# Two triples side by side in the first product of a ConvNeXt block, with another order of loads, pads and norms

## The chip, the cores and the metric

The kernel runs on one core of one Trainium2 chip. The metric is the device time of one execution in microseconds (us); smaller is better. Times of the kernel before are given as the median of three runs.

## The reference

All data are fp32. The input x is (32, 384, 28, 28): 32 images (here called blocks, b), C = 384 channels, 784 pixels. Two layers follow each other:

```python
# layer 0: ConvNeXt block
y = depthwise_conv_7x7(x, dw_w) + dw_b            # padding 3
y = layernorm over the 384 channels of a pixel
y = gelu(y @ w1 + b1)                             # 384 -> 1536, exact gelu
gx = sqrt(sum over pixels of y * y)               # per image and feature
nx = gx / (mean of gx over the features + 1e-6)
y = grn_g * (y * nx) + grn_b + y                  # GRN
x = x + (y @ w2 + b2)                             # 1536 -> 384
# layer 1: a gate for each channel
avg, mx, mn = mean, max, min of x over the pixels
logits = concat(avg @ W1.T, grouped(mx, W2_1) * W2_2, mn @ W3.T) @ Wfc.T
out = sigmoid(logits + x)
```

GRN needs the sum of squares over all pixels of a block before any of its features can be scaled, so within a block the second product has to wait for the whole first product.

## The kernel before

**Convolution stage (0 to 497.6 us).** x is read in 12 chunks of 32 channels. A chunk consists of eight pieces (`NG = 8`), each of 32 channels by 4 images: 128 partitions of 784 pixels, 0.4 MB. `load_x(i)` issues the load of piece i, `AHEAD = 6` pieces before it is needed. `pad_x(i)` copies it into a buffer with rows padded to 32 (GpSimd, L245). `turn_x` transposes the padded piece on TensorE (L256) and copies the transposes into the chunk's tile xt (VectorE L264, ScalarE L266). The convolution itself is a product of xt with a banded matrix per channel. These matrices are not stored: the DRAM table `fs` holds one short row per channel (written at the start, L200 and L207, on ScalarE's DMA queue), and `load_t(s)` (L211) reads it with a skewed access pattern into `tmat`, 8 channels per step s, 48 steps in all, four `tmat` buffers. TensorE makes `pc` from both (L393, L394, L397), VectorE (L403) and ScalarE (L411) add the bias `dwb` and write `yc`, which goes to DRAM (`yd`, `yl`). Beside each step the next chunk's pieces are padded and transposed. GpSimd also forms sums of weights in this stage and stores them in `u1d` and `u2d`.

**Products.** Both products use a bilinear scheme with 15 block products where a plain 3 x 3 x 2 product takes 18. The operands are blocks and sums of blocks: `forms_up` (L573) makes the sums for the first product, `forms` (L679) for the second, both on GpSimd after the first block. The table `UPSTEPS` lists the 15 steps of the first product: the operand, the weight sum, the PSUM bank, whether the bank is started anew, and what is done with the bank afterwards (a copy on ScalarE or an add, subtract or reversed subtract on VectorE). `up(b)` goes through four triples of 128-feature rows, `KT = 4`; a triple is 15 steps on two matmul instructions each (L607), and its six results (copies L614, sums L616 to L624) are the halves of three rows of y. It loads the triple's weights in one piece of 960 KB (L596), two buffers. `down(b)` is the second product: 15 steps of eight matmul instructions (L703), weights from L698, and VectorE adds each bank to x (L717, L719).

**What runs beside them.** Per block there are 12 `gelu` (L582), 12 `square` (L588) with the sums of squares, one `grn` (L637 to L649), 12 `scale` on ScalarE, and for the block that comes after next `turn`: for each of seven pixel tiles j a norm on ScalarE (`yn`, L515), three transposes on TensorE (`py`, L533), and after tiles 3 and 6 three evictions on ScalarE that apply the LayerNorm's weights (`acc`, L515). `stats` and `std` prepare the norms, `gate_store` (L738 to L757) does the gate of the block before.

**Order.** After `up(0)` and `up(1)` comes `down(0)`, and then `up(b + 1)` and `down(b)` alternate. A dictionary of hooks says at which step of a product another function is called. Within `up` a `gelu` stands after steps 3, 7 and 11 of a triple (for the triple before it) and a `square` after the same steps from the third triple on (for the one two before it). `beside(b)` gives the hooks of `down(b)`: the last three `gelu` at step 0, `turn` of b + 2 at steps 0 to 3, six `square` at 4 and 5, `stats`, `std` and `grn` at 8, `gate_store` and `load_x` at 9, the scales at 10 to 13, `forms` at 14. `start_hooks()` does the same for `up(0)` and `up(1)`. The order of the calls is the order of the instructions on each engine, and an engine takes its instructions in that order. SP issues nearly all loads and stores; ScalarE's queue issues the stores of `fs` and of `out`.

A step is defined like this:

```python
    ("z", "-12", "D", 1, (("D", "add", "2b"),)),
    ("0b", "-10+11", "A", 0, (("A", "copy", "1b"), ("D", "rsub", "1b"))),
```

Step z writes bank D, which VectorE adds to the half row 2b; step 0b goes on in bank A, which ScalarE copies to 1b, and then VectorE subtracts 1b from bank D.

Of the kernel before, what the change touches and what calls it, by code (L numbers as in the profile page):

```python
# [89 lines left out]

UPSTEPS = (
# [8 lines left out]
    ("z", "-12", "D", 1, (("D", "add", "2b"),)),  # L100
    ("0b", "-10+11", "A", 0, (("A", "copy", "1b"), ("D", "rsub", "1b"))),
    ("0a", "-00", "B", 0, (("B", "sub", "0a"),)),
    ("t", "+00+10-11", "H", 1, (("H", "add", "E"),)),
    ("q", "-00+01+02-10+11", "A", 0, (("A", "plus", "0b"),)),
    ("u", "+00+10+12", "B", 0, (("B", "minus", "1a"),)),
    ("2b", "-12-20+21+22", "F", 1, (("F", "add", "2b"),)),
)
KT = FB // 3

# [10 lines left out]
def convnext_gate_kernel(  # L120
# [26 lines left out]
    fs = dram.tile([C + 1, FL], F32, name="fs")  # L147
# [28 lines left out]
    with ExitStack() as one:  # L176
        tp = one.enter_context(tc.tile_pool(name="tp", bufs=1))
        xip = one.enter_context(tc.tile_pool(name="xip", bufs=6))
# [21 lines left out]
        nc.scalar.dma_start(fs[C : C + 1, :], tab[:1, 0, :])  # L200
        for cb in range(CB):
            nc.vector.tensor_copy(
                tab[:, cb, S0 : S0 + SN - 7].rearrange("p (y x) -> p y x", x=PW)[:, :, :7],
                dww[:, cb, :42].rearrange("p (y x) -> p y x", x=7),
            )
            nc.vector.tensor_copy(tab[:, cb, S0 + SN - 7 :], dww[:, cb, 42:])
            nc.scalar.dma_start(fs[cb * P : (cb + 1) * P, :], tab[:, cb, :])  # L207
        NK = C // TC

        def load_t(s, eng=nc.sync):  # L210
            eng.dma_start(  # L211
                tmat[s % NT2].rearrange("p c m -> p (c m)"),
                bass.AP(
                    tensor=fs.tensor,
                    offset=fs.offset + s * TC * FL,
                    ap=[[1, P], [1, TC * FL]],
                ),
            )
# [25 lines left out]
        def pad_x(i):  # L244
            nc.gpsimd.tensor_copy(  # L245
                xpad[i % NPAD][:, :, :HW], xis.pop(i).rearrange("p (r w) -> p r w", w=HW)
            )
# [80 lines left out]
        AHEAD = 6  # L328
# [3 lines left out]
        for i in range(NG):  # L332
            pad_x(i)
            if i == NG - AHEAD:
                load_t(0)
            if i == NG // 2:

                nc.gpsimd.tensor_copy(tmat[1][:, 0, :1], xpad[i % NPAD][:, 0, :1])
                load_t(1)
                nc.sync.dma_start(dwb, cvec[0:1, :].broadcast_to([P, C]))  # L340
            if i + AHEAD < GT:
                load_x(i + AHEAD)
            for h in range(2):
                turn_x(i, h, xt, (nc.vector, nc.scalar)[h])
# [116 lines left out]
    up1 = ctx.enter_context(tc.tile_pool(name="up1", bufs=2))  # L461
# [15 lines left out]
    ssqs, gscs, gates, ys, ops = {}, {}, {}, {}, {}  # L477
# [39 lines left out]
    def turn(b, j, norm=nc.scalar, evac=(nc.scalar,) * CB):  # L517

        rstd, nmr = sts[b]
        h = j // 4  # L520
        if j == 0:

            pool, tag = (xp, "x") if b == 1 else (accp, "acc")
            accs[b] = pool.tile([P, CB, NT], F32, tag=tag, name=f"acc_{b}")
        if j % 4 == 0:
            pts[b] = [bank(f"py_{b}_{h}_{cb}") for cb in range(CB)]
        yn = ynp.tile([P, C], F32, tag="yn", name=f"yn_{b}_{j}")
        affine(
            norm, yn.rearrange("p (k c) -> p k c", c=YC), yis[b][:, :, j, :],
            rstd[:, j : j + 1], nmr[:, j : j + 1],  # L530
        )
        for cb in range(CB):
            nc.tensor.transpose(  # L533
                pts[b][cb][:, j % 4 * P : (j % 4 + 1) * P], yn[:, cb * P : (cb + 1) * P], ident
            )
        if j % 4 < 3 and j < NJ - 1:
            return
        for cb in range(CB):
            affine(
                evac[cb],  # L540
                accs[b][:, cb, h * 4 * RW * HW : (j + 1) * RW * HW].rearrange(
                    "p (r w) -> p r w", w=HW
                ),
                pts[b][cb][:, : (j % 4 + 1) * P]
                .rearrange("p (j q) -> p j q", q=P)[:, :, ::-1]
                .rearrange("p j (r w) -> p j r w", w=PW)[:, :, :, :HW],
                lng_t[:, cb : cb + 1],
                lnb_t[:, cb : cb + 1],
            )
# [40 lines left out]
    def up(b, hooks, squares=True):  # L590
# [3 lines left out]
        for t in range(KT):  # L594
            wt = up1.tile([P, NS, P], F32, tag="u1", name=f"u1_{b}_{t}")
            nc.sync.dma_start(wt, u1d[t])  # L596
            banks = {}
            z = {
                f"{m}{'ab'[h]}": ym[:, 3 * t + m, h * NH : (h + 1) * NH]
                for m in range(3)  # L600
                for h in range(2)
            }
            z["E"] = tep.tile([P, NH], F32, tag="te", name=f"te_{b}_{t}")
            for i, (opnd, _, bk, first, acts) in enumerate(UPSTEPS):
                if first:
                    banks[bk] = bank(f"ph_{b}_{t}_{bk}")
                nc.tensor.matmul(  # L607
                    banks[bk][:, :NH], wt[:, i, :], o[opnd],
                    start=(first == 1), stop=True, skip_group_check=True,
                )  # L610
                for src, how, to in acts:
                    p, d = banks[src][:, :NH], z[to]
                    if how == "copy":
                        nc.scalar.activation(d, p, AF.Identity)  # L614
                    elif how == "add":
                        nc.vector.tensor_tensor(d, d, p, ALU.add)  # L616
                    elif how == "sub":
                        nc.vector.tensor_tensor(d, d, p, ALU.subtract)  # L618
                    elif how == "rsub":
                        nc.vector.tensor_tensor(d, p, d, ALU.subtract)  # L620
                    elif how == "plus":
                        nc.vector.tensor_tensor(d, p, z["E"], ALU.add)  # L622
                    else:
                        nc.vector.tensor_tensor(d, p, z["E"], ALU.subtract)  # L624
                if i in (3, 7, 11):
                    m = (i - 3) // 4
                    if t >= 1:
                        gelu(b, 3 * (t - 1) + m)
                    if t >= 2 and squares:
                        square(b, 3 * (t - 2) + m)  # L630
                run(hooks, (t, i))
# [131 lines left out]
    def beside(b):  # L763
# [4 lines left out]

        n = b + 1
        last = n == B - 1  # L770
        if n < B:
            for m in range(3):
                at(0, gelu, n, FB - 3 + m)
# [6 lines left out]
        if n < B:  # L780
            f0 = 0 if b == 0 else FB - 6
            for i in range(f0, FB):
                at((i - f0) // 3 if last else 4 + (i - f0) // (2 if b else 4), square, n, i)
        if b + 3 < B:
            at(8, stats, b + 3)
            at(8, std, b + 3)
        if n < B:
            at(2 if last else 8, grn, n)
        if b >= 1 and not last:
            at(9, gate_store, b - 1)  # L790
        if n < B:
            at(9 if b else 0, load_x, n)
        if n < B:
            for f in range(FB):
                at((2 if last else 10) + f // 3, scale, n, f)
            if last:
                at(6, forms, n, 0, 4)
                at(9, forms, n, 4, EARLY)
            else:
                at(NS - 1, forms, n, 0, EARLY)  # L800
        if b >= 1 and last:
            at(7, gate_store, b - 1)
        return hooks

    def start_hooks():
        h0, h1 = {}, {}

        def at(h, t, i, fn, *args):  # L810
            h.setdefault((t, i), []).append(lambda: fn(*args))

        V, A = nc.vector, nc.scalar
        if B > 1:
            at(h0, 0, 8, stats, 1)
            at(h0, 0, 8, std, 1)
            for j in range(NJ):
                at(h0, 1, 1 + 2 * j, turn, 1, j, V)
            at(h0, 1, NS - 1, forms_up, 1)
        if B > 2:  # L820
            at(h0, 2, 6, load_y, 2)
        for m in range(3):
            at(h1, 0, 1 + 2 * m, gelu, 0, FB - 3 + m)
        for i in range(6):
            at(h1, i // 5, (8, 10, 11, 12, 13, 0)[i], square, 0, FB - 6 + i)
        if B > 2:
            at(h1, 0, 5, stats, 2)
        at(h1, 1, 1, grn, 0)
        if B > 2:
            at(h1, 1, 1, std, 2)  # L830
        for f in range(FB):
            at(h1, 1 + (6 + f) // 12, (6 + f) % 12, scale, 0, f, A if f % 2 else V)
        at(h1, 2, 8, forms, 0, 0, EARLY)
        return h0, h1

    h0, h1 = start_hooks()
    stats(0)
    std(0)
    for j in range(NJ):
        turn(0, j, (nc.scalar, nc.vector)[j % 2], (nc.scalar, nc.vector, nc.scalar))  # L840
    forms_up(0, nc.vector)
    if B > 1:
        load_y(1)
    up(0, h0)
    load_x(0)
    if B > 1:
        up(1, h1, squares=False)
    else:
        for fs in h1.values():
            for fn in fs:  # L850
                fn()
    for b in range(B):
        if b >= 1 and b + 1 < B:
            up(b + 1, {})
# [41 lines left out]
```

## Time and profile before

| | |
|---|---|
| Time, median of 3 runs | 3168.45 us (3166.55 to 3168.86) |
| Profiled execution: time | 3168.3 us |
| Profiled execution: span | 3166.6 us |
| Busy in the span: PE, DVE, ACT, POOL | 3125.4, 1685.1, 1878.7, 1616.9 us |
| Convolution stage | 0 to 497.6 us |
| Change of stage | 497.6 to 512.5 us |
| One steady block | 82.57 us: first product 40.32, second product 42.25 |

PE is TensorE's matmul, PEld its weight load, DVE is VectorE, ACT is ScalarE, POOL is GpSimd, and SP issues transfers. L12 is line 12 of the kernel. The page of the profile gives busy time per engine, the chain of work that ended last, and groups of instructions. A stage window sums one stretch of time: for each engine the sum of durations and the number of instructions, then the granted TensorE clock (1.00 is full), the mean busy share of the DMA engines, and what they moved in GB/s. A timeline lists single instructions or runs of like ones: start in us from the span's start, duration in us, engine, line, operation, output <- inputs, shape, and xN for a run of N. What stands in brackets at its end is idle time of the engine ahead of it, with what ended it.

### The profile page before, as it was taken

To read this page: it belongs to the slowest core of one execution; us is meant where nothing else is said; L and a number is where in the kernel's file an instruction comes from. 1 tells how busy PE (TensorE), PEld (TensorE's weight loads), DVE (VectorE), ACT (ScalarE), POOL (GpSimd) and SP (SyncE) were. 2 spreads that over 40 slices of the span, in tenths; PEclk is the share of its full clock that TensorE was granted. 3 is DMA by queue.
4 is the path that set the end of the run, shared out by engine and by line. 5 is a ranking of instruction groups with operands and counts; after the bars stand their busy time and mean duration, and the time that the engine had idled before them with its cause. 6 is when DMAs were issued, how large, how long until landed. Compare 5 with 4: busy or idle time off the path is not lost.

```text
span 3166.6 us, 33843 instructions
## 1 busy us (share of the span) xinstructions
PE 3125.4 (99%) x11459; PEld 1978.5 (62%) x11459; DVE 1685.1 (53%) x3444; ACT 1878.7 (59%) x3032; POOL 1616.9 (51%) x853
## 2 busy tenths in 40 slices
PE   8999998999999999999999999999999999999998
PEld 7999996555555555555555555555555555555554
DVE  3443436555555555555555555555555555555554
ACT  2222225866677766666666666666666666677762
POOL 2453421555555555555555555555555555555555
PEclk9999999999999999999999999999999999999999
DMA  9989985434444444444444444444444444444333
GB/s 346 356 311 395 348 302 191 132 114 143 143 144 142 134 137 145 143 136 148 148 136 148 145 138 147 136 148 148 148 130 137 132 145 144 143 142 144 127 102 131
DMA packets 257154, 540.73 MB, mean 171 GB/s; under 512 B 121022, under 2 KB 130775, under 8 KB 247767
## 3 DMA queue, kind: packets, MB, share of 16 engines
q1 hardware_dynamic: 244148, 500.70, 47.2%
q10 hardware_dynamic: 12834, 37.88, 3.1%
q8 instruction: 91, 1.49, 0.2%
q14 instruction: 81, 0.66, 0.1%
HBM read 447.53 MB, written 90.99 MB: 170 GB/s over the span
## 4 chain that ended last, share of the span: by engine, by line
PE 98%; DVE 1%; ACT 1%; DMA 1%; issue 0%; ACTq 0%; POOL 0%; POOLq 0%; SPq 0%; DVEq 0%
PE ph_A L607 14%; PE ph_B L607 13%; PE pz_A L703 11%; PE pz_B L703 11%; PE pz_C L703 5%; PE ph_C L607 5%; PE pz_E L703 5%; PE pc L393 5%; PE pc L394 4%; PE pc L397 4%; PE pz_F L703 3%; PE ph_D L607 3%; PE ph_H L607 3%; PE ph_F L607 3%; PE pz_G L703 3%; PE pz_D L703 3%
## 5 line engine op out<-in xcount | busy, mean ns | idle before, releaser
L582 ACT ACTIVATE y<-y,fv 128x784 f32<-128x784 f32 x384 | 346.8, 941 | 214.2 <-DVE y L622 213.5
L679 POOL TENSOR_TENSOR d_v<-d_u,y 128x1568 f32<-128x1568 f32 x32 | 112.3, 3509 | 661.2 <-PE pz_B L703 640.6
L515 ACT ACTIVATE y<-y,fv,gsc 128x784 f32<-128x784 f32 x378 | 358.7, 1027 | 30.1 <-DVE gsc L649 30.1
L588 ACT ACTIVATE junk<-y 128x784 f32<-128x784 f32 x384 | 326.6, 851 | 5.0
L411 ACT ACTIVATE yc<-pc,dwb 128x224 f32<-128x224 f32 x192 | 103.6, 641 | 367.4 <-PE pc L397 269.8
L607 PE MATMUL ph_A<-af,u 128*128 128x392 f32 x768 | 313.8, 503 | 5.4 <-DVE af L573 5.3
L607 PE MATMUL ph_B<-af,u 128*128 128x392 f32 x768 | 311.3, 493 | 0.3 <-ACT y L614 0.3
L703 PE MATMUL pz_A<-y,u 128*128 128x392 f32 x768 | 268.5, 492 | 0.0
L738 POOL TENSOR_TENSOR zt<-gate,st 128x96 f32<-128x96 f32 x32 | 11.2, 350 | 456.9 <-DVE st L726 456.9
L679 POOL TENSOR_TENSOR y<-d_v,y 128x1568 f32<-128x1568 f32 x64 | 223.5, 3514 | 2.4
L607 PEld LDWEIGHTS ph_A<-af,u 128*128 128x128 f32 x768 | 136.4, 190 | 135.2 <-ACT y L614 57.7
L607 PE MATMUL ph_A<-acc,u 128*128 128x392 f32 x512 | 216.3, 504 | 0.0
L393 PE MATMUL pc<-xt,tmat 128*128 128x224 f32 x768 | 209.4, 354 | 6.3 <-issue 4.5
L607 PE MATMUL ph_B<-acc,u 128*128 128x392 f32 x512 | 213.6, 499 | 0.0
L607 PEld LDWEIGHTS ph_B<-af,u 128*128 128x128 f32 x768 | 145.2, 190 | 109.0 <-DVE y L618 9.6
L703 PEld LDWEIGHTS pz_A<-y,u 128*128 128x128 f32 x768 | 145.8, 190 | 106.6
L245 POOL COPY xpad<-xi 128x784 f32<-128x784 f32 x96 | 80.5, 839 | 250.7 <-PE pt L256 178.6
L618 DVE TENSOR_TENSOR y<-y,ph_A 128x392 f32<-128x392 f32 x128 | 71.9, 562 | 238.3 <-PE ph_A L607 227.3
L504 ACT ACTIVATE sd<-mv,eps_t 128x7 f32<-128x7 f32 x32 | 9.6, 300 | 314.3 <-DVE mv L499 314.3
L614 ACT ACTIVATE y<-ph_A 128x392 f32<-128x392 f32 x256 | 123.9, 484 | 112.7 <-PE ph_A L607 112.6
L573 POOL TENSOR_TENSOR af<-af,acc 128x392 f32<-128x392 f32 x186 | 187.1, 1019 | 4.9
L397 PE MATMUL pc<-xt,tmat 128*128 128x192 f32 x768 | 187.6, 326 | 0.0
(157 smaller groups left out, 7043.1 us busy)
## 6 DMA issues: line engine op xcount, KB each, us to landing
u<-u1d SPq DMA_DIRECT2D x128, 960.0 KB, 4.7
u<-u2d SPq DMA_DIRECT2D x480, 256.0 KB, 2.6
tmat<-fs SPq DMA_DIRECT2D x48, 1420.0 KB, 11.2
yd<-yc SPq DMA_DIRECT2D x22, 1792.0 KB, 8.8
yi<-yd SPq DMA_DIRECT2D x32, 1232.0 KB, 6.5
xi<-in_x SPq DMA_DIRECT2D x96, 392.0 KB, 9.5
x<-in_x SPq DMA_DIRECT2D x32, 1176.0 KB, 6.1
out<-x ACTq DMA_DIRECT2D x31, 1176.0 KB, 5.1
```

Of the source, the lines that this page charges most:

```text
L393: nc.tensor.matmul(pc[:, ci, :N], t[:, c, P : 2 * P], xc, start=True, stop=False)
L394: nc.tensor.matmul(pc[:REACH, ci, : N - B], t[:, c, 2 * P : T0 + MW], xc[:, B:], start=False, stop=False)
L397: nc.tensor.matmul(pc[:, ci, B:N], t[:, c, :P], xc[:, : N - B], start=False, stop=True)
L411: nc.scalar.activation(yc[:, :, :, cy + ci].rearrange("p b j -> p j b"), pc[:, ci, :N].rearrange("p (j b) -> p j b", j=NJ), AF.Identity, b ...
L515: eng.activation(out, in_, AF.Identity, bias=add, scale=mul)
L573: eng.tensor_tensor(d, o[in0], o[in1], op)
L582: nc.scalar.activation(y, y, AF.Gelu, bias=b1_t[:, f : f + 1], scale=1.0)
L588: nc.scalar.activation(junk, ys[b][:, f, :], AF.Square, accum_out=ssqs[b][:, f : f + 1])
L607: nc.tensor.matmul(banks[bk][:, :NH], wt[:, i, :], o[opnd], start=(first == 1), stop=True, skip_group_check=True,)
L614: nc.scalar.activation(d, p, AF.Identity)
L679: nc.gpsimd.tensor_tensor(d, o[in0], o[in1], op)
L703: nc.tensor.matmul(pz[:, :NH], wt[:, t, :], o[opnd][:, t, :], start=(first == 1 and t == 0), stop=(t == KT - 1), skip_group_check=True,)
```

## The change

**Start of the convolution stage.** x is loaded eight pieces ahead, in eight buffers, where it was six. `fs` becomes three tables, one for each 128 channels, each with its own extra row; a `load_t` therefore depends on the stores to one table. The first `load_t` comes in two halves right after the first pad, with the load of `dwb` behind it, and the second `load_t` two pieces before the end of the first chunk. From the ninth piece on `pad_x` is an activation (Identity) on ScalarE.

```diff
-        xip = one.enter_context(tc.tile_pool(name="xip", bufs=6))
+        xip = one.enter_context(tc.tile_pool(name="xip", bufs=8))
...
-            nc.gpsimd.tensor_copy(
-                xpad[i % NPAD][:, :, :HW], xis.pop(i).rearrange("p (r w) -> p r w", w=HW)
-            )
+            if i < NG:
+                nc.gpsimd.tensor_copy(dst, src)
+            else:
+                nc.scalar.activation(dst, src, AF.Identity)
...
-        AHEAD = 6
+        AHEAD = NG
...
-            if i == NG - AHEAD:
-                load_t(0)
-            if i == NG // 2:
+            if i == 0:
+                load_t(0, 2)
+                nc.sync.dma_start(dwb, cvec[0:1, :].broadcast_to([P, C]))
+            if i == NG - 2:
```

**First product.** The steps of triples t and t + 1 alternate. Each of the two triples has three banks A, B and C: steps z, t and 2b, which had banks of their own (D, H and F), now go through C. The weights of a triple come in three loads of 5 steps (320 KB each), six buffers.

```diff
-    ("z", "-12", "D", 1, (("D", "add", "2b"),)),
-    ("0b", "-10+11", "A", 0, (("A", "copy", "1b"), ("D", "rsub", "1b"))),
+    ("z", "-12", "C", 1, (("C", "add", "2b"),)),
+    ("0b", "-10+11", "A", 0, (("A", "copy", "1b"), ("C", "rsub", "1b"))),
...
-    ("t", "+00+10-11", "H", 1, (("H", "add", "E"),)),
+    ("t", "+00+10-11", "C", 1, (("C", "add", "E"),)),
...
-    ("2b", "-12-20+21+22", "F", 1, (("F", "add", "2b"),)),
+    ("2b", "-12-20+21+22", "C", 1, (("C", "add", "2b"),)),
...
+        for t2 in range(0, KT, 2):
             for i, (opnd, _, bk, first, acts) in enumerate(UPSTEPS):
...
+                for t in (t2, t2 + 1):
+                    if i % UG == 0:
+                        wts[t] = up1.tile([P, UG, P], F32, tag="u1", name=f"u1_{b}_{t}_{i}")
+                        nc.sync.dma_start(wts[t], u1d[t, :, i : i + UG, :])
```

**What runs beside the products.** `norm` is split from `turn`; the norms of tiles 0 and 1 of block b + 1 are called within `up(b)`, near its end, and `turn` uses them later. The scales and the `forms` of a block leave the end of its `down` neighbour and are called in the first pair of triples of the next `up`. The first six `gelu` of a block stand in the second pair of triples, the other six in the first two steps of `down`, and the squares from step 3. `stats` stays at 8; `std` and `grn` go to 9, `gate_store` and `load_x` to 10. The first two blocks and the last have orders of their own.

```diff
+        else:
+            for i, f in enumerate(order):
+                at((0, 2 * i), scale, p, f)
+            at((0, 24), forms, p, 0, EARLY)
+        if b != 1:
+            for m in range(HF):
+                at((2, 2 + 4 * m), gelu, b, m)
+            for m in range(squared(b)):
+                at((2, 28 if m >= HF // 2 else 22 + 2 * m), square, b, m)
+        if 1 <= b and b + 1 < B:
+            for j in range(2):
+                at((2, 26 + 2 * j), norm, b + 1, j)
...
-            f0 = 0 if b == 0 else FB - 6
-            for i in range(f0, FB):
-                at((i - f0) // 3 if last else 4 + (i - f0) // (2 if b else 4), square, n, i)
+            g0 = 0 if n == 1 else HF
+            for f in range(g0, FB):
+                at((f - g0) // 3, gelu, n, f)
+            s0 = squared(n)
+            for f in range(s0, FB):
+                at((1 if last else 3) + (f - s0) // 2, square, n, f)
...
-            for f in range(FB):
-                at((2 if last else 10) + f // 3, scale, n, f)
-            if last:
-                at(6, forms, n, 0, 4)
-                at(9, forms, n, 4, EARLY)
-            else:
-                at(NS - 1, forms, n, 0, EARLY)
+        if last:
+            for i, f in enumerate(order):
+                at(4 + i // 3, scale, n, f)
+            at(8, forms, n, 0, 4)
+            at(9, forms, n, 4, EARLY)
```

`p` is b - 1, `n` is b + 1, `HF` is 6, `order` is the rows of y with each third row last, and a key (2, m) is the m-th of the 30 steps of the second pair of triples.

## Prediction of the time

> **What bounds the kernel now.** I read the busy table and the chain that ended last first, then the stage windows, then single timelines. One profiled execution has a span of 3166.6 us and a time of 3168.3 us (1.7 us lie around the span); the median of the runs is 3168.45, so the sums below are made against 3168.3 and hold for the median too.
>
> The page, parts 1 and 4:
>
> ```profile
> PE 3125.4 (99%) x11459; PEld 1978.5 (62%) x11459; DVE 1685.1 (53%) x3444; ACT 1878.7 (59%) x3032; POOL 1616.9 (51%) x853
> PE 98%; DVE 1%; ACT 1%; DMA 1%; issue 0%; ACTq 0%; POOL 0%; POOLq 0%; SPq 0%; DVEq 0%
> ```
>
> TensorE (PE) is the bound from end to end. Work on another engine counts only where TensorE waits for it. Now one steady block, first product (120 matmul instructions), then second product (120, with 21 transposes and the two small sums), in the stage windows:
>
> ```profile
> 1384.02:1424.34 40.32, 40.32 (x121) 22.04 (x120) 25.59 (x48) 27.53 (x51) 24.89 (x8) 1.00 0.30 108
> 1424.34:1466.60 42.26, 42.26 (x147) 25.31 (x146) 20.62 (x51) 28.20 (x40) 20.36 (x13) 1.00 0.55 174
> ```
>
> Both show PE busy for the whole window, but records overlap, so a short wait hides in them. The starts in TensorE's timeline show it:
>
> ```profile
> 1420.02 0.82 PE L607 MATMUL ph_H<-af,u 128*128 128x392 f32 x2
> 1420.75 0.93 PE L607 MATMUL ph_A<-acc,u 128*128 128x392 f32 x2
> 1421.52 0.82 PE L607 MATMUL ph_B<-acc,u 128*128 128x392 f32 x2
> 1422.27 0.93 PE L607 MATMUL ph_A<-af,u 128*128 128x392 f32 x2
> 1423.03 0.82 PE L607 MATMUL ph_F<-acc,u 128*128 128x392 f32 x2
> ```
>
> An unhindered pair of instructions takes 0.658 us to the next start (eight in 2.63). Here the steps are 0.73, 0.77, 0.75 and 0.76: a bank is reused before ScalarE or VectorE has read it, and a resumed matmul reads 0.93 in place of 0.82, about 0.1 us of restart. A first product without such waits takes 60 x 0.6583 = 39.50 us, so **0.82 us per block** is lost. The second product loses 0.2.
>
> At the start of the kernel, TensorE's timeline again:
>
> ```profile
> 14.17 0.98 PE L256 MATMUL pt<-ident,xpad 128*128 128x128 f32 x7 [0.21 <-POOL xpad L245]
> 21.82 3.68 PE L256 MATMUL pt<-ident,xpad 128*128 128x128 f32 x16 [6.67 <-POOL xpad L245]
> 25.65 0.71 PE L393 MATMUL pc<-xt,tmat 128*128 128x224 f32 x2 [0.15 <-ACT xt L266]
> ```
>
> The seventh piece of x is late by 6.67 us, because it stands behind tmat's 1420 KB in the queue. The convolution starts at 25.65.
>
> **What the Trainium skill says.** "Trainium Kernel Development and Optimization", Performance Expectations: matmul busy time is a bad metric, since matmuls are pipelined. The trace agrees: 100% busy above, with 0.82 us lost. "PSUM — Partial Sum Buffer", Engine vs sequencer instructions: ScalarE's, VectorE's and GpSimd's queues are strict FIFO, and matmuls start in program order. That licenses the queue walk below; nothing in the trace speaks against it. "ScalarE: Activation LUTs", What ACT_TABLE_LOAD costs: an ACTIVATE with immediate operands costs 186 ns + 0.833 ns per element, so 0.84 us for a pad of 784. The trace has 0.84 for GpSimd's pad, and 0.48 for ScalarE's copy of 392 where the formula gives 0.51.
>
> **The change, part by part.**
>
> *Start.* Eight pieces of x are issued before tmat, tmat comes in two halves, and it waits for the first fs store alone. By 12.9 us the queue now lands six pieces (2.41 MB) and the stores. In the built program the fifth load waits for the second to land (7.3 us by its pad), about 2 us later than now; the last two pieces are 0.8 MB, 2 us at the 417 GB/s that the transfer view shows near 20 us. So the eighth lands near 15; pad 0.84, transposes 0.8, eviction 0.7: 17.5. The first half of tmat (0.73 MB) follows x, near 17. First pc at 17.5, **8.1 us earlier**. Then the ninth piece stands behind tmat's halves and dwb and lands near 20.6; ScalarE's pad makes it 21.5, where TensorE wants it at 19.5: 2 us back. Net **-6**, bounds -8 and 0 (nothing, if tmat's fs store is slowed by x's loads).
>
> *Pads on ScalarE.* 88 pads x 0.84 = 74 us move from GpSimd to ScalarE, which is at 102.6 of 469 us in this stage: hidden. Each pad stands ahead of evictions in ScalarE's queue; four pc buffers, 9.8 us of work, cover it. If a load were late by more, TensorE would wait that much. x is loaded eight ahead in place of six, which should take away the one late piece near 253 us (TensorE lost 1.6). **-1.5**, bounds -3 and +3. The change of stage (497.6 to 512.5) keeps its steps.
>
> *First product.* The same 60 matmul pairs, copies and sums. Steps of triples t and t+1 alternate, so a bank has twice the time. Two costs come with it. (a) z, t and 2b share bank C, so t waits for VectorE's rsub of 1b, behind ScalarE's copy. For the second pair of triples: 0b (step 48) starts at 31.6, is visible 0.86 later (q at 1422.27 is read at 1423.23, less the restart), copy 0.48, rsub 0.57: 33.6, and t (step 52) wants it at 34.2. No wait, margin 0.6; the first pair, with the scales of the block before between the copies, has the same margin. (b) Weights come as 384 loads of 320 KB in place of 128 of 960: eight more issues of about 0.35 us on SP per block, in a window with DMA at 0.30 to 0.55; six buffers put them 13 us ahead of use, against 4.7 us to land. Hidden; a late one would cost up to 4.7. So **-0.82 per block**.
>
> *What is moved beside it.* Per block still 12 gelu, 12 squares, 12 scales, 7 norms, all on ScalarE. Scales go from the second product's end to the next first product. GpSimd's forms start about a microsecond later (7 x 3.5 us, end near 29), and their first reader comes at 46: hidden. But all six gelu of the second pair of triples now fall at the end of the first product, where three stood, and three squares instead of one stand ahead of the norm of tile 5. ScalarE and TensorE here now:
>
> ```profile
> 1423.83 2.63 ACT L582 ACTIVATE y<-y,fv 128x784 f32<-128x784 f32 x3 [1.62 <-DVE y L622]
> 1428.18 1.29 ACT L515 ACTIVATE yn<-yi,nmr,rstd 128x384 f32<-128x384 f32 x2
> 1431.74 1.94 ACT L515 ACTIVATE acc<-py,cv 128x448 f32<-128x448 f32 x3
> 1433.57 1.30 ACT L515 ACTIVATE yn<-yi,nmr,rstd 128x384 f32<-128x384 f32 x2
> ```
> ```profile
> 1434.55 0.49 PE L533 MATMUL py<-ident,yn 128*128 128x128 f32 x3
> ```
>
> Tile 5's norm ends at 1434.27 and its transposes start at 1434.55: 0.28 us to spare. After the change, in us from the block's start: q of the third triple (step 54) starts at 35.55, is read at 36.41, summed by 36.98. ScalarE's queue in the built order: six gelu at a pitch of 0.84, from 37.0 to 42.1; a square 0.86; two norms 1.20; three squares 2.80; three acc evictions 1.83; norm of tile 5, 0.70: **49.45**. The table load that stands here now goes behind it. TensorE starts the second product at 39.50 and, since these transposes now stand ahead of pz_E (0.66 earlier), wants tile 5 at 39.50 + 10.20 - 0.66 = **49.04**. It waits 0.4, and 0.1 to restart, say 0.52, bounds 0 and 2. Queued behind are the second product's matmuls alone; they have slack for nothing else.
>
> Net per steady block -0.82 + 0.52 = **-0.30; x 29 = -8.7**. First two blocks and their joint: now about 3 us of waits; -1, bounds +2 and -3. Tail: the last block's scales are issued two steps later, but its forms still start near 20 us into the second product: 0, bounds 0 and +2.
>
> Sum: -6 - 1.5 - 8.7 - 1 = -17; 3168.3 - 17 = **3151**.
>
> **The rivals.** *Norms in time* (A): ScalarE is ahead by 0.5, all of the 0.82 stays: -24 - 8.5, so 3136. For it: queue pitches overlap. Against: each is read from the trace. *ScalarE becomes the bound at the joint of the products* (B): the norm of tile 5 comes 1.3 us later still, the size of one table load (1.28): wait 1.9, net +1.06 x 29 = +31, less 8.5: 3191. It turns slower than before once the wait is over 0.82 + 8.5 / 29 = 1.1 us. For it: one FIFO, nothing but transposes in front. Against: the walk. *The start gives nothing* (C): x's eight loads delay the store that tmat waits for, or ScalarE's pads hold evictions: 3168.3 - 9.7, so 3159, and 3165 with half of the steady gain.
>
> **How the numbers follow.** Forecast 0.50 (own range 3143 to 3161), A 0.15, C 0.15, B 0.20. Some 0.2% (6 us) is what a measurement of this kernel can tell from no change. Faster: 0.48 + 0.15 + 0.05 = 0.68; same 0.10; slower 0.20 + 0.02 = 0.22. Leaving out B and little else, the range is 3134 to 3170.
>
> **What would show it.** Right: first pc near 17.5 and a short wait for ScalarE's xpad after it; first products at 39.5; tile 5's transposes waiting some 0.4 us for yn in every block; blocks at 82.3 in place of 82.57. Wrong: waits of ph_C's matmul for VectorE, a wait for a u1 load, or a yn wait of over 1.1 us.

## The result, and the profile after

The median goes from 3167.97 us (3166.55 to 3168.86, 7 runs) to **3158.31 us** (3157.46 to 3159.83, 7 runs); the ratio is 0.997, with a 95% interval of 0.9959 to 0.9982. The kernel is 9.7 us faster, where 17 were forecast; 3158.31 lies in the stated range. The profiled execution took 3159.22 us with a span of 3157.5.

Parts 1 and 4 of the page of the kernel after:

```profile
PE 3108.3 (98%) x11459; PEld 2001.5 (63%) x11459; DVE 1679.4 (53%) x3446; ACT 1948.7 (62%) x3116; POOL 1545.0 (49%) x765
PE 86%; ACT 11%; DVE 2%; issue 1%; DMA 1%; ACTq 0%; POOLq 0%; DVEq 0%; SPq 0%
```

TensorE still bounds the kernel, but ScalarE now holds 11% of the chain, where it held 1%: in each block the chain leaves TensorE for a stretch of ScalarE's queue, from the six gelu to a norm. The same steady block in the stage windows, first product, then second product:

```profile
1382.06:1421.56 39.50, 39.50 (x122) 22.80 (x121) 26.24 (x48) 28.67 (x48) 24.88 (x8) 1.00 0.38 128
1421.56:1464.30 42.74, 42.46 (x146) 25.34 (x145) 19.52 (x51) 27.13 (x42) 20.36 (x13) 1.00 0.52 155
```

The first product takes 39.50 us, with nothing lost; the second takes 42.74, half a microsecond more than before. Where that half microsecond lies is in two timelines of the joint. ScalarE first, then TensorE:

```profile
1419.07 5.14 ACT L596 ACTIVATE y<-y,fv 128x784 f32<-128x784 f32 x6 [3.40 <-DVE y L642]
1424.12 0.84 ACT L602 ACTIVATE junk<-y 128x784 f32<-128x784 f32 x1
...
1424.96 1.29 ACT L523 ACTIVATE yn<-yi,nmr,rstd 128x384 f32<-128x384 f32 x2
1426.15 0.84 ACT L602 ACTIVATE junk<-y 128x784 f32<-128x784 f32 x1
...
1428.96 1.94 ACT L523 ACTIVATE acc<-py,cv 128x448 f32<-128x448 f32 x3
1430.78 1.30 ACT L523 ACTIVATE yn<-yi,nmr,rstd 128x384 f32<-128x384 f32 x2
```
```profile
1430.77 0.49 PE L547 MATMUL py<-ident,yn 128*128 128x128 f32 x3
1431.54 0.55 PE L547 MATMUL py<-ident,yn 128*128 128x128 f32 x3 [0.28 <-ACT yn L523]
```

Tile 4's transposes start at 1430.77; tile 5's would follow 0.33 later, at 1431.10 (49.04 us after the block's start at 1382.06). The norm of tile 5 is the first of the two at 1430.78; the second begins 0.60 later, and a norm takes 0.70, so the first ends near 1431.48. TensorE starts at 1431.54 instead of 1431.10: 0.44 us, and the first transpose after a wait reads longer (0.55 us for the three in place of 0.49). The waits of TensorE from 520 us to the end (who waits, for whom, us in total, times, longest) show that it is in all 29 steady blocks, and is the only wait that repeats:

```profile
PE py L547 <- ACT yn L523: 8.0, 29, 0.3
PE pa L754 <- POOL zt L752: 3.1, 1, 3.1
```

Of the start, TensorE's timeline (the rows of L402 and L405, and some of L401, are left out):

```profile
17.41 0.98 PE L264 MATMUL pt<-ident,xpad 128*128 128x128 f32 x7 [0.16 <-POOL xpad L253]
18.98 0.65 PE L401 MATMUL pc<-xt,tmat 128*128 128x224 f32 x2 [0.58 <-ACT xt L274]
...
20.11 0.54 PE L401 MATMUL pc<-xt,tmat 128*128 128x224 f32 x2
...
21.93 0.66 PE L264 MATMUL pt<-ident,xpad 128*128 128x128 f32 x4 [0.63 <-ACT xpad L255]
```

The convolution starts at 18.98, not 25.65; then the ninth piece is late, and TensorE stands for 0.63 us until 21.93.

So the steady blocks did what was forecast. The convolution did not. The table follows the starts of TensorE's matmuls in both profiled executions (step 3 is the fourth of the 48 steps); the last column is the part of the difference that arises in that stretch:

| Start of | before | after | after - before | arises here |
|---|---|---|---|---|
| step 3 of the convolution | 54.89 | 49.84 | -5.05 | -5.05 |
| last pc | 497.24 | 498.87 | +1.63 | **+6.68** |
| first product of block 0 | 512.46 | 513.35 | +0.89 | -0.74 |
| first product of block 2 | 641.01 | 641.86 | +0.85 | -0.04 |
| last two second products | 3075.78 | 3066.45 | -9.33 | -10.18 |
| end of the span | 3166.6 | 3157.5 | -9.1 | +0.23 |

The start gains 5 us and the stage gives back 6.7. What in the convolution takes them is the question of the experiments.

### The profile page after: what moved, and what is told of

Read it like the earlier page. It is cut to its first block, busy times and chain, and to the rows that moved or that the text cites. A ratio compares the mean times of both kernels' runs of the same rounds, so it can differ in the third digit from the quotient of the medians.

```text
span 3157.5 us, 34396 instructions
## 1 busy us (share of the span) xinstructions
PE 3108.3 (98%) x11459; PEld 2001.5 (63%) x11459; DVE 1679.4 (53%) x3446; ACT 1948.7 (62%) x3116; POOL 1545.0 (49%) x765
## 4 chain that ended last, share of the span: by engine, by line
PE 86%; ACT 11%; DVE 2%; issue 1%; DMA 1%; ACTq 0%; POOLq 0%; DVEq 0%; SPq 0%
PE ph_A L627 13%; PE ph_B L627 12%; PE ph_C L627 12%; PE pz_A L717 11%; PE pz_B L717 8%; PE pz_E L717 5%; PE pz_C L717 5%; ACT y L596 5%; PE pc L401 5%; PE pc L402 4%; PE pc L405 4%; PE pz_F L717 3%; ACT junk L602 3%; ACT acc L523 2%; ACT yn L523 2%; PE pt L264 2%
## 5 line engine op out<-in xcount | busy, mean ns | idle before, releaser
L627 PE MATMUL ph_A<-af,u 128*128 128x392 f32 x768 | 287.0, 496 | 6.0 <-DVE af L587 5.4
L627 PE MATMUL ph_B<-af,u 128*128 128x392 f32 x768 | 285.6, 494 | 0.0
L627 PE MATMUL ph_C<-af,u 128*128 128x392 f32 x768 | 284.4, 493 | 0.0
L636 DVE TENSOR_TENSOR y<-y,ph_C 128x392 f32<-128x392 f32 x384 | 216.1, 563 | 31.8 <-PE ph_C L627 1.0
L627 PEld LDWEIGHTS ph_A<-af,u 128*128 128x128 f32 x768 | 146.3, 191 | 113.9 <-DVE af L587 5.6
L401 PE MATMUL pc<-xt,tmat 128*128 128x224 f32 x768 | 210.1, 355 | 6.2 <-DVE yc L411 1.8
L627 PEld LDWEIGHTS ph_C<-af,u 128*128 128x128 f32 x768 | 146.0, 190 | 107.7 <-DVE y L640 1.6
L411 DVE TENSOR_TENSOR yc<-pc,dwb 128x448 f32<-128x448 f32 x96 | 89.8, 937 | 188.4 <-PE pc L405 154.7
L627 PE MATMUL ph_A<-acc,u 128*128 128x392 f32 x512 | 189.6, 492 | 0.0
L627 PE MATMUL ph_C<-acc,u 128*128 128x392 f32 x512 | 189.6, 492 | 0.0
L627 PE MATMUL ph_B<-acc,u 128*128 128x392 f32 x512 | 189.5, 492 | 0.0
```

The costliest lines, as they stand in the source:

```text
L401: nc.tensor.matmul(pc[:, ci, :N], t[:, c, P : 2 * P], xc, start=True, stop=False)
L627: nc.tensor.matmul(banks[t, bk][:, :NH], wts[t][:, i % UG, :], o[opnd], start=(first == 1), stop=True, skip_group_check=True,)
```

## The experiments

Each time below is a median, with the ratio to the kernel before on the same chip and its 95% interval. On all the chips used the kernel before takes 3167.8 to 3168.1 us.

### Which half of the change: runs 1 and 2

The two kernels share the change out at one line of the code: the part up to the end of the convolution stage from one kernel, all that follows from the other.

> The convolution stage, its loads and pads as before; first product, hooks and their order as after. Theory (the gain comes from the products alone): the change of stage ends at 512.5 as before, first products take 39.50, second products 42.75 with one wait of about 0.45 us ahead of tile 5's transposes, so a block takes 82.25 in place of 82.57: -0.33 x 29 = -9.6, in all about 3158. Rival (the products gain less, and the start's gain of 6.7 us at the first pc is still in the sum): about 3165.

> Convolution stage as after (eight pieces ahead, three tables, pads on ScalarE), products as before. Theory: first pc near 19.0, but the stage ends near 498.9, and the whole takes 3168 + 0.9 = 3169. Rival (the start's gain reaches the end): 3162.

Measured: products alone **3157.4** (0.9968, 0.9955 to 0.998); convolution alone **3168.7** (1.0004, 0.9996 to 1.0012). All of the gain comes from the products, and the convolution stage as changed brings nothing. In its own profile its first pc is at 17.93, yet its last is at 497.00, against 497.24 before.

### The pads on ScalarE: run 3

```diff
-            if i < NG:
-                nc.gpsimd.tensor_copy(dst, src)
-            else:
-                nc.scalar.activation(dst, src, AF.Identity)
+            nc.gpsimd.tensor_copy(dst, src)
```

> The kernel after with all pads of x on GpSimd. Theory (a pad on ScalarE waits for one of two xpad buffers, and evictions behind it in the queue wait with it): the 6 us of extra waits between 140 and 466 us vanish, the first pc stays near 19, the stage ends near 493 and the time is about 3152. Rival (the DMA engines, 0.9 to 1.0 busy up to 430 us, set the end of the stage): waits for late pieces of x or stores of yc take the place, the stage ends near 498, time 3158. In both the wait for the ninth piece near 21 us stays.

Measured: **3163.7** (0.9986, 0.9979 to 0.9992), 5 us slower than the kernel after. Both theories fall: the pads' place on ScalarE is not what costs; with this order it saves. The waits of TensorE from 20 to 490 us in this run:

```profile
PE pt L261 <- POOL xpad L252: 8.7, 5, 3.0
PE pc L398 <- issue: 4.0, 8, 1.1
PE pt L261 <- DVE xt L269: 2.5, 6, 0.4
PE pc L398 <- DVE yc L408: 1.8, 1, 1.8
```

The same in the kernel after:

```profile
PE pt L264 <- DVE xt L272: 3.9, 9, 0.4
PE pc L401 <- DVE yc L411: 1.8, 1, 1.8
PE pc L401 <- ACT xpad L255: 1.4, 3, 0.6
PE pc L401 <- DVE xt L272: 1.4, 4, 0.3
PE pc L401 <- issue: 1.1, 1, 1.1
PE pt L264 <- ACT xpad L255: 0.9, 2, 0.6
```

No load is named in either ("issue" is a wait for which the profile names nobody), and the small waits are at the same steps in both (12, 14 to 16, 18, 20 and from 35 to 40), whichever engine pads. What both kernels share is TensorE's order. Between 186 and 204 us the kernel before has its transposes in groups of four and three with pc matmuls between, and TensorE doesn't wait:

```profile
191.21 0.60 PE L256 MATMUL pt<-ident,xpad 128*128 128x128 f32 x4
191.65 0.55 PE L393 MATMUL pc<-xt,tmat 128*128 128x224 f32 x2
...
193.71 0.49 PE L256 MATMUL pt<-ident,xpad 128*128 128x128 f32 x3
```

The kernel after has this, in TensorE's timeline:

```profile
189.85 1.25 PE L264 MATMUL pt<-ident,xpad 128*128 128x128 f32 x10
191.54 0.94 PE L264 MATMUL pt<-ident,xpad 128*128 128x128 f32 x6 [0.44 <-DVE xt L272]
```

The second half of one piece, all of the next and nearly all of the one after it stand in a row, and the row breaks after the third pt tile (3 + 4 + 3 transposes), when the three pt banks are full; then VectorE's copy is awaited. In the built program's queue this concerns pieces 11, 35, 39, 43, 47, 51, 55, 83, 87 and 91: the first half of each, or a part of it, stands three quarters of a step ahead of where it is called, in some the second half with it, right behind the piece before, which stands ahead too (the expectation of run 5 says half a step, which is the distance to the piece before). In the kernel before the longest row is ten transposes, three pt tiles, at the end of a chunk. The section on the kernel before says that the order of the calls is the order of the instructions; that was too simple, since in the built queue the scheduler has moved instructions that are independent.

### What brings that order: runs 5 to 7

Run 5 is run 1 with one thing more, the lookahead:

```diff
-        xip = one.enter_context(tc.tile_pool(name="xip", bufs=6))
+        xip = one.enter_context(tc.tile_pool(name="xip", bufs=8))
...
-        AHEAD = 6
+        AHEAD = NG
```

> The products as after; the convolution stage as before but for x being loaded eight pieces ahead (eight buffers) in place of six; pads on GpSimd, tmat and its tables as before. The transposes of pieces 35, 39, 43, 47, 51, 55, 83, 87 and 91 stand half a step earlier in TensorE's queue, right behind those of the piece before. Theory (this order costs the start's gain: a piece's pad can't start before the transposes of two pieces earlier have freed the xpad buffer): waits of about 0.6 us and more at these pieces, between 140 and 230 and between 365 and 450 us, and the stage ends 6 us or more later than with six ahead: about 3163. Rival (pads on ScalarE, or the tables, cost the gain): as with the products alone, 3157.

Measured: **3165.5** (0.9993, 0.9984 to 1.0001), 8 us more than run 1, although its first pc comes at 19.82 us instead of 24.74. In its profiled execution (span 3161.0 us, one of the quickest of this kernel) the last pc is at 501.44 instead of 496.49. Loading eight ahead is alone enough for both an early start and the loss. The loss is larger here than in the kernel after, as in run 3, whose pads are on GpSimd as well: TensorE's waits for xpad are 6.3 us in four places, and those for VectorE's copies, which lead in the kernel after, 2.1:

```profile
PE pt L258 <- POOL xpad L247: 6.3, 4, 2.9
PE pt L258 <- DVE xt L266: 2.1, 5, 0.4
```

The edit has a side effect: load_t(0) stands at the piece `NG - AHEAD`, so it moves from the third pad to the first. That moves no transposes: in run 6 it is at the first pad too, and its queue has none of these rows.

Run 6 is the kernel after with eight loads at the beginning and six ahead from then on:

```diff
-        AHEAD = NG
-        for i in range(AHEAD):
+        AHEAD = 6
+        for i in range(NG):
...
-            if i + AHEAD < GT:
+            if NG <= i + AHEAD < GT:
```

> The kernel after, with the first eight pieces loaded at once and from the ninth on six ahead. The transposes stand in TensorE's queue as in the kernel before. Theory: the waits at pieces 35 to 91 go, first pc near 18, the ninth piece's wait of 2 us stays, the stage ends about 5 us before that of the products alone (496.5): about 3152. Rival (ScalarE's pads hold evictions in any order, or the DMA engines set the end): the stage ends near 498, 3158.

> As the run before it, with all pads on GpSimd. Theory (what runs the pads does not matter while they stand in this order): 3152 as well, within 1 us. Rival (GpSimd's sums of weights stand ahead of pads, as the waits of 3.1 and 1.8 us at steps 18, 20 and 38 in the run with all pads on GpSimd show): 2 to 5 us more.

Measured: **3152.6** for both (0.9952, 0.9939 to 0.9966; 0.9954, 0.9941 to 0.9966). The last pc is at 490.93 with ScalarE's pads and at 491.47 with GpSimd's. The early start is kept to the end, 5 us ahead of run 1 as expected, and in this order it makes no difference which engine pads. The waits of run 6 from 20 to 490 us:

```profile
PE pc L401 <- DVE xt L272: 3.0, 9, 0.3
PE pc L401 <- DVE yc L411: 1.5, 1, 1.5
PE pc L401 <- issue: 1.1, 1, 1.1
PE pt L264 <- ACT xpad L255: 0.7, 1, 0.7
```

The waits of transposes for copies are gone; nine waits of 0.3 us at the ends of chunks stay, as in the kernel before (whose profile names nobody for them). Why the scheduler moves these pieces when eight loads are ahead isn't shown by any run.

### What makes that order dear: runs 9 to 11

Two things could make the row cost: the two xpad buffers (a pad waits for the transposes of two pieces before), and the three PSUM banks for pt. Runs 9 and 10 are the kernel after and run 3 with a third xpad buffer; the table's source lies in another buffer to make room.

```diff
-        tab = tp.tile([P, CB, FL], F32, name="tab")
+        tab = ws[:, : CB * FL].rearrange("p (cb m) -> p cb m", m=FL)
...
-        NPAD = 2
+        NPAD = 3
```

> The kernel after (eight pieces ahead, pads on ScalarE) with three xpad buffers in place of two; the table's source tab lies in a part of ws that is not yet used, to make room. The transposes of pieces 39, 43, 47, 51, 55, 83, 87 and 91 keep their early place in TensorE's queue. Theory (their pad waits for the transposes of two pieces earlier to free the buffer): with a third buffer the pad is made a piece earlier, the waits of about 0.6 us at these pieces go, the stage ends near 494 and the time is about 3153. Rival (the early place itself costs, through the transposes' PSUM banks and their copies on VectorE): 3158 as after.

> As the run before it, with all pads on GpSimd (against 3163.7 with two buffers). Theory: the waits of 3.1, 1.8 and 1.8 us at steps 18, 20 and 38 come from GpSimd making a sum of weights first because the pad's buffer was not free; with a third buffer they go too, about 3154. Rival (GpSimd is late with these pads in any case): 3160 or more.

Measured: **3157.3** (0.9968, 0.9956 to 0.998) with ScalarE's pads and **3158.6** (0.9971, 0.9959 to 0.9982) with GpSimd's. Run 9 went the rival's way: 1 us, and its built queue has one row less, at piece 35. In its timelines a row breaks as in the kernel after, though no pad is awaited in it; TensorE, then VectorE:

```profile
189.13 1.26 PE L264 MATMUL pt<-ident,xpad 128*128 128x128 f32 x10
190.82 0.94 PE L264 MATMUL pt<-ident,xpad 128*128 128x128 f32 x6 [0.44 <-DVE xt L272]
```
```profile
189.33 0.96 DVE L411 TENSOR_TENSOR yc<-pc,dwb 128x448 f32<-128x448 f32 x1 [1.37 <-PE pc L405]
190.14 2.19 DVE L272 COPY xt<-pt 128x384 f32<-128x384 f32 x4
```

VectorE is still at an eviction of yc (0.96 us) when the first pt tile is full, and the copies follow it. Run 10 went the theory's way, but for 5 us of the nearly 10 forecast: with GpSimd the long waits for xpad do come from the buffer, and the waits for VectorE's copies stay. Its waits for xpad, from 20 to 490 us, are down from 8.7 us in five to the ninth piece's alone:

```profile
PE pt L261 <- DVE xt L269: 3.4, 8, 0.4
PE pc L398 <- DVE yc L408: 1.8, 1, 1.8
PE pt L261 <- POOL xpad L252: 1.6, 1, 1.6
```

Run 11 goes on from run 9 with another split of the PSUM banks:

```diff
-        psx = one.enter_context(tc.tile_pool(name="psx", bufs=3, space=bass.MemoryType.PSUM))
-        psc = one.enter_context(tc.tile_pool(name="psc", bufs=4, space=bass.MemoryType.PSUM))
+        psx = one.enter_context(tc.tile_pool(name="psx", bufs=4, space=bass.MemoryType.PSUM))
+        psc = one.enter_context(tc.tile_pool(name="psc", bufs=3, space=bass.MemoryType.PSUM))
```

> Three xpad buffers as in the run with three xpad buffers and ScalarE's pads, and of the eight PSUM banks four for the transposes pt and three for pc, in place of three and four. In TensorE's queue 17 pieces (not 8) now have their transposes right behind those of the piece before. Theory (14 transposes in a row fill three pt banks, and the fourth waits for VectorE's copy, which stands behind an eviction of yc): four banks take the whole row, the waits of 0.4 us and the restart of 0.1 go at all of these pieces and at the ends of the chunks, about 4 to 8 us: 3150 to 3153. Rival (a row of transposes costs the same with any number of banks): 9 more rows at 0.6 us, 3162. Three pc banks may cost something of their own: then waits of pc for evictions on ScalarE or VectorE appear.

Measured: **3152.3** (0.9949, 0.9935 to 0.9962). About twice as many pieces stand in rows, and the kernel is 5 us faster than run 9. A row now runs through:

```profile
207.80 2.14 PE L264 MATMUL pt<-ident,xpad 128*128 128x128 f32 x15
209.78 0.55 PE L401 MATMUL pc<-xt,tmat 128*128 128x224 f32 x2
```

The last pc is at 491.58, nearly as early as in run 6. (The expectation counted 14 transposes in a row; with the half piece ahead of them there are up to 17.) Run 11 also has more rows than run 9, but steps 18 to 21 hold the same transposes in both: from the start of step 18 to that of step 22 run 9 takes 40.47 us and run 11 39.73, 0.37 less for each of two rows.

One measure goes through all of these runs: the time from the start of step 3 to that of the last pc, in the profiled execution.

| Kernel | Loads ahead | Pads (from the ninth piece) | xpad buffers, pt banks | us |
|---|---|---|---|---|
| before; run 1 | 6 | GpSimd | 2, 3 | 442.35; 442.34 |
| run 6; run 7 | 8, then 6 | ScalarE; GpSimd | 2, 3 | 442.17; 442.24 |
| run 2 | 8 | ScalarE | 2, 3 | 447.34 |
| after | 8 | ScalarE | 2, 3 | 449.03, with half clock in step 23 |
| run 3; run 5 | 8 | GpSimd | 2, 3 | 451.96; 451.90 |
| run 9; run 10 | 8 | ScalarE; GpSimd | 3, 3 | 446.62; 446.57 |
| run 11 | 8 | ScalarE | 3, 4 | 442.22 |

So the order costs 5.0 us with pads on ScalarE (run 2 less the kernel before) and 9.6 on GpSimd. A third xpad buffer takes back 0.7 or 5.4 of it, and a fourth pt bank beside it, tried with ScalarE's pads, the other 4.4.

### The half microsecond at the joint: run 4

```diff
-        nc.scalar.activation(junk, ys[b][:, f, :], AF.Square, accum_out=ssqs[b][:, f : f + 1])
+        if f == 7:
+            y = ys[b][:, f, :]
+            nc.vector.scalar_tensor_tensor(
+                junk, y, 1.0, y, ALU.mult, ALU.mult, accum_out=ssqs[b][:, f : f + 1]
+            )
+        else:
+            nc.scalar.activation(junk, ys[b][:, f, :], AF.Square, accum_out=ssqs[b][:, f : f + 1])
```

> The kernel after with one of the twelve squares of each block (f = 7) on VectorE. Theory (tile 5's norm is late because of what stands ahead of it in ScalarE's queue): 0.86 us less stands ahead of it, and in the built order the three acc evictions go behind it, so it ends about 47.0 us after the block's start, 2 us before TensorE wants it: the second product takes 42.25, -0.5 x 29 = -14.5, about 3144. Rival (the wait is the transposes' own, or VectorE's longer queue delays the sums of the second product): no gain, 3158 or more.

Measured: **3143.8** (0.9924, 0.9912 to 0.9937), 14.5 us less than the kernel after. In the built order the norm of tile 5 now stands alone ahead of the three acc evictions, in ScalarE's timeline of the same block:

```profile
1423.94 0.69 ACT L524 ACTIVATE yn<-yi,nmr,rstd 128x384 f32<-128x384 f32 x1
1424.54 1.93 ACT L524 ACTIVATE acc<-py,cv 128x448 f32<-128x448 f32 x3
```

The wait for yn is gone from all 29 blocks; TensorE's waits from 520 us to the end are one:

```profile
PE pa L761 <- POOL zt L759: 3.1, 1, 3.1
```

Second products take 42.25 us again and first products 39.50. What stood ahead of tile 5's norm was the cause, and VectorE had room for a square. How much of the relief is the square and how much the evictions isn't separated.

### Both together: runs 8 and 12

> Eight pieces at once and then six ahead, and one square per block on VectorE. The two gains lie in different stages and should add: 3152 - 14.5 = 3138. If they don't add, the sum of the two single runs' differences to the kernel after is missed by over 2 us.

Measured: **3137.8** (0.9905, 0.9892 to 0.9919). The differences to the kernel after, -5.7 and -14.5, sum to -20.2; the two together give -20.6. They add. This beats both kernels: 30 us less than before.

> The combined kernel (eight pieces at once, then six ahead; one square per block on VectorE; two xpad buffers) with four pt banks and three pc banks. In TensorE's queue only the transposes of the second piece of each chunk move. Theory: the waits of 0.5 us at the end of each chunk go: 10 x 0.5 = 5 us less than 3137.8 at most, some 3134. Rival (the pads, or three pc banks, wait in their place): 3138 or more.

Measured: **3138.0** (0.9904, 0.989 to 0.9917). No gain: the rival holds. The waits for VectorE's copies at the ends of the chunks are gone but for one, and waits for pads take their place, from 20 to 500 us:

```profile
PE pt L265 <- ACT xpad L256: 3.6, 10, 1.5
PE pc L402 <- DVE yc L412: 2.1, 1, 2.1
```

With two xpad buffers the bank taken from pc buys nothing. Run 11 had three; this kernel with three was not run.

## Why the prediction was right, and where not

**First product: right.** -0.82 per block was forecast from the starts of the matmuls; they are 39.50 apart in place of 40.32. No ph_C waits for VectorE and no u1 load is late. "100% busy" stood over both, as the Trainium skill's "Trainium Kernel Development and Optimization" (Performance Expectations) warns; pitches between starts told the loss.

**Second product: right, to 0.03 us.** The walk through ScalarE's queue put tile 5's norm at 49.45 us and TensorE's need at 49.04; the trace has some 49.42 and 49.04. A wait of 0.52 was taken; the block shows 0.49. That rests on the strict order of ScalarE's queue, which the Trainium skill states ("PSUM — Partial Sum Buffer", Engine vs sequencer instructions); the trace agrees, and run 4 confirms it: with one square less, and acc evictions behind the norm, the wait is nought. Rival A (no wait) and B (1.9 us) are out.

**Steady sum: right.** -8.7 forecast, -10.18 measured: 30 first products gain 24.5 (0.82 each, the first 0.71) and 29 second products lose 14.3 (0.49 each): -10.2. Taking 29 of each missed one first product, 0.8.

**Start: nearly right.** -6 forecast, -5.05 by step 3. First pc came at 18.98 instead of 17.5, and the ninth piece's wait is there. The two misses hang together: in the convolution-only run the first pc is at 17.93, yet step 3 starts at 49.67, so that piece, and not the first pc, seems to set the pace.

**The rest of the convolution: wrong.** -1.5 was forecast, with bounds of -3 and +3; it is +6.68. Two steps failed. The late spot near 253 us was read as a late piece of x that eight loads ahead would cure. Before, GpSimd's pad does wait 3.58 us for a load there, but TensorE's own wait is for VectorE. After, no load is late there, and that wait stays. Before, the pad and TensorE's wait (from the list of waits from 250 to 256 us), then after:

```profile
251.26 0.84 POOL L245 COPY xpad<-xi 128x784 f32<-128x784 f32 x1 [3.58 <-DMA xi<-in_x]
PE pc L393 <- DVE yc L403: 1.6, 1, 1.6
```
```profile
254.79 1.02 PE L401 MATMUL pc<-xt,tmat 128*128 128x224 f32 x2 [1.75 <-DVE yc L411]
```

What holds VectorE there was not tried.

And the lookahead was costed as a change in the loads alone. It moved the transposes in TensorE's queue, and that order costs 5.0 of the 6.68, 4.4 of it through the three pt banks; runs 1, 2, 5, 6, 9 and 11 show it. In the bounds, late loads and pads on ScalarE were thought the dangers; no load is late here, and the pads cost nothing (run 7 against 6). The other 1.7 is the clock: TensorE was granted half of it for 3.4 us from 254.9, and step 23 took 10.01 us where it takes 8.33 in the profile of the convolution-only run. Whether every execution of the kernel has this stretch isn't known. An estimate by the formula in the Trainium skill's "ScalarE: Activation LUTs" (What ACT_TABLE_LOAD costs) gave 0.84 us for a pad of 784 elements on ScalarE; the trace has 0.857.

**Which case it was.** That the total lies in the forecast's range is in part luck. One term missed by 8.2 us and left its own bounds; the misses of the others, 1.5 us at most, nearly cancel, and the range of the total was just wide enough. In time, rival C ("the start gives nothing", 3159) was nearer than the forecast. Its mechanisms are out, though: x's loads didn't hold the store that tmat waits for, since the first pc came 6.7 us earlier, and ScalarE's pads weren't the cost. **First blocks and tail:** -1 forecast for the first blocks, -0.04 measured; the change of stage, costed at 0, gained 0.74; the tail lost 0.23.

## What to carry to other kernels

The wait at the joint was foretold to a tenth of a microsecond by walking the strict queues from measured durations, and one instruction moved to an idler engine then removed it: try such a walk before building. An edit of buffers or lookahead can change the order of instructions that it doesn't name: compare the queues of the bound engine before costing it, and ask of every new row of like instructions whether its banks are emptied in time. Here an early start counted only where every later stretch kept its pace, so follow the difference of the two traces from step to step to where it is lost.

## What was not expected of the hardware

The half-clock stretches of TensorE lie differently from kernel to kernel though the work is the same: before, 6.8 us from 19.0, where TensorE waited until 21.82 and then took 3.68 us for 16 transposes; after, none at the start, where seven transposes take 0.98 us, but 3.4 us from 254.9, right behind a wait of 1.75 us, at a cost of 1.7 us. At the pace of those seven the 16 would take some 2.2 us (an estimate), so about 1.4 us of what the start gained by its first pc may be the clock and not the loads. The convolution-only run has the same wait and no half clock there, nor has run 9 behind 1.79 us. The run with one square on VectorE, whose convolution stage is that of the kernel after, has it at the same place. What decides it was not tried.
